# Two cross-attentions on one core: four products of the first output pair put beside the last attention subtiles, its bias added by VectorE, and two kinds of transfer changing queues

## The chip, the core and the metric

The kernel runs on one core of one Trainium2 chip. A core has TensorE (PE in the profile, with its weight loads as PEld), VectorE (DVE), ScalarE (ACT), GpSimd (POOL) and SyncE (SP, which here only issues transfers); sixteen DMA engines move data between the core's on-chip memory and the chip's main memory (DRAM). Every engine takes its own instructions strictly in order and waits on semaphores for the others. A transfer is issued by an instruction of some engine's queue, so a transfer that has to wait also holds up what stands behind it in that queue. The metric is the device time of one execution in microseconds (us), lower is better.

## The reference

Two cross-attention layers run one after the other over x of 4 x 1024 rows of 1024 numbers, float32, with a context of 64 rows for each batch item:

```python
# layer 0: 32 query heads of 32, 8 key heads, then a layer norm
q = hidden_state @ Wq + bq
scores = einsum('bkgld,bksd->bkgls', q, k) * scale + mask
attn = softmax(scores)
out = einsum('bkgls,bksd->bkgld', attn, v)  ->  (b, l, 1024)
out = out @ Wo + bo
x = out + hidden_state
return (x - mu) * rsqrt(var + EPS) * gamma + beta
# layer 1: 16 heads of 64, keys and values from the normalized context
Q = hidden_states @ Wq.T ; K = a @ Wk.T ; V = a @ Wv.T
out = softmax(Q K^T * scale) V
return hidden_states + tanh(gate) * (out @ Wo.T)
```

## The kernel before, in words

The 4096 rows are cut into 32 subtiles of 128 rows (`t`), four blocks of eight subtiles (`blk`), and 16 pairs of subtiles (`pair`). The large products (1024 x 1024 weights) are done by a scheme of seven products of half-size blocks instead of eight, so each needs sums of blocks of its two factors first: `right_sums` (L179) makes those of a weight, `left_out` (L417) makes S1, S2, S4 and, in place, S3 of a pair of subtiles with four VectorE operations. `project` (L428) runs the seven products of a pair: each is four matmuls of 128x128 by 128x512 (L436) into one of the four PSUM banks `wx`, followed by an addition of the bank into the rows `r` by VectorE (L444). Several products run on in one bank (X), so the next of them waits for the addition that reads the bank. Between the products `project` takes steps from the list `fill`.

The program has these stages.

1. Keys and values of the context, and the queries of block 0 (up to about 200 us of the profile).
2. Attention of layer 0, subtile by subtile, in `mix` (L764). A subtile has its scores (`front`, L676 on TensorE and L680 on VectorE, twice), the maxima (L687), the subtraction (L690), the exponentials (L702), the sums and reciprocals (L707, L708), the division (L711), a transposition of the probabilities, and the products with the values (`values`, L752), whose result is stored to `oTd` (L758). For subtiles from 19 on, the transposition is done by TensorE (`turn`, L406) with a copy by ScalarE (L407). Queries are loaded a subtile ahead into two buffers (`load_queries`, L643, with the mask at L647), from SP's queue.
3. Beside the attention, `mix` takes steps of `other_work` (L950) at five places of a subtile. For subtiles 0 to 23 these are the query products of the next blocks. For the last eight subtiles they are the *folded query weights* of layer 1: for each of eight chunks `k`, `turned_chunk` (L875) loads a chunk of the turned weight `wq1T` (on GpSimd's queue, L877), and four steps of `folded_queries` (L880) multiply it with the keys (L890), copy the result by ScalarE (L896) and, after each second step, store 1 MB of it to `ad` (on SP's queue, L902). Eight of the 32 steps are run ahead of subtile 24; the other 24 are three for each subtile. During chunks 1 to 4 the weight `wo` of layer 0's output is loaded; after chunk 5 its sums are made and `load_outputs(0)` (L933) loads pair 0's attention output `o2_0` and its two tiles of rows of x, to which **GpSimd** adds the bias `bo` (L946). When all steps are done, `left_out` makes pair 0's sums.
4. The output stage: a loop over the 16 pairs (L1069) runs `project` with `wo`. Its `fill` holds, for pairs 0 to 7, the *folded values* of layer 1 (`folded_values`, L908: L917 on TensorE, L922 on ScalarE, stores at L926), the closing layer norm of the pair before (`close_rows`, L1028), and in pair 0 first what is left of subtile 31 (its transposition and `values`) and `open_stage` (L1013), which gives the memory of the attention pools to the output stage's pools (`left`, `o2`, `res`, `const2`). Rows of later pairs get their bias from GpSimd (L946).
5. Layer 1, pair by pair (from about 1150 us), with no part in the change.

The order inside an engine is set by a scheduler from program order and from what each step needs, except where `keep_in_program_order` pins an instruction. The pool `wpool` has seven buffers of the tag `wb` that are used in rotation; from chunk 0 on, the chunks of `wq1T` and the two result tiles `a_k_0`, `a_k_1` of each chunk take turns in them, so a chunk's load waits for the store of a result tile of two to three chunks before (L877 and L902 depend on each other in this way).

Of the kernel before, what the change touches and what calls it, by code (L numbers as in the profile page):

```python
# [8 lines left out]
F32 = mybir.dt.float32  # L9
# [5 lines left out]
P = 128  # L15
# [56 lines left out]
def tile_two_cross_attentions(  # L72
# [352 lines left out]
        nc.vector.tensor_tensor(s["S4"], a12, s["S2"], ALU.subtract)  # L425
        return {"A11": a11, "A12": a12, "A22": a22, "S3": a21, **s}

    def project(a, w, r, fill, bias=None, tail=None):  # L428

        fresh = set()

        def product(bank, s, m, first, last):
            for k in range(HK):
                nc.tensor.matmul(  # L436
                    bank, a[s][:, k, :], w[m][:, k, :],
                    start=first and k == 0, stop=last and k == HK - 1, skip_group_check=True,
                )

        def add(u, n, bank):
            at = r[u][:, n * 512 : (n + 1) * 512]
            if bias is None or (u, n) in fresh:
                nc.vector.tensor_tensor(at, bank, at, ALU.add)  # L444
            else:
                fresh.add((u, n))
                at = at.rearrange("p (h s) -> p h s", s=S)
                nc.vector.tensor_tensor(  # L448
                    at, bank.rearrange("p (h s) -> p h s", s=S),
                    bias.unsqueeze(1).to_broadcast([P, 512 // S, S]), ALU.add,  # L450
                )

        share = -(-len(fill) // 7)

        def others():
            for _ in range(min(share, len(fill))):
                fill.pop(0)()

        X, V = wx(), wx()
        product(X, "A11", "B11", True, False)  # L460
        add(0, 0, X)
        others()
        product(X, "S2", "T2", False, False)
        add(1, 0, X)
        others()
        product(V, "S3", "T3", True, False)
        add(1, 1, V)
        others()
        product(X, "S1", "T1", False, False)
        add(1, 1, X)  # L470
        others()
        product(X, "S4", "B22", False, True)
        add(0, 1, X)
        others()
        if tail:
            tail()
        product(V, "A22", "N4", False, True)
        add(1, 0, V)
        others()
        W = wx()  # L480
        product(W, "A12", "B21", True, True)
        add(0, 0, W)
        others()

    def softmax_front(s, floor, name, late=False):
        mx = small.tile([P, 16], F32, tag="mx", name=f"mx_{name}")
# [387 lines left out]

    def turned_chunk(k):  # L875
        t = wpool.tile([P, KC, P], F32, tag="wb", name=f"wq1T_{k}")
        nc.gpsimd.dma_start(out=t, in_=wq1T[k])  # L877
        return t

    def folded_queries(kT, wT, k):  # L880

        st = [wpool.tile([P, B, 512], F32, tag="wb", name=f"a_{k}_{n}") for n in range(2)]

        def heads(cc):
            banks = [wx(), wx()]
# [14 lines left out]
            if cc % 2:  # L900
                n = cc // 2
                nc.sync.dma_start(  # L902
                    out=ad[:, sub_ap(k), n * 512 : (n + 1) * 512].rearrange("b p o -> p b o"), in_=st[n]
                )

        return [lambda cc=cc: heads(cc) for cc in range(4)]

    def folded_values(vT, wch, c):  # L908
# [21 lines left out]

        return [lambda bp=bp: keys(bp) for bp in range(2)]

    def load_outputs(pair):  # L933
        o = (o2pool if pair else early).tile([P, KC, 2 * P], F32, tag="o2", name=f"o2_{pair}")
        load = nc.sync.dma_start(out=o, in_=oTd[pair])
        if not pair:
            tc.keep_in_program_order(load)
        r = []
        for u in range(2):
            t = pair * 2 + u  # L940
            ru = (rpool.tile([P, H], F32, tag="r", name=f"r_{t}") if pair
                  else early.tile([P, H], F32, tag="r", name=f"r_{t}", bufs=2))
            load = nc.sync.dma_start(out=ru, in_=x[sub_ap(t), :])
            if not pair:
                tc.keep_in_program_order(load)
            nc.gpsimd.tensor_tensor(ru, ru, bo_sb, ALU.add)  # L946
            r.append(ru)
        return o, r

    def other_work(rows):  # L950

        nonlocal fold, early, bo_sb, w_o, first_outputs
        for blk in range(1, NBLK):
            steps = query_steps(blk, rows)
            fills = {}
# [30 lines left out]
        first_outputs = left_out(o, early, "0_0"), r  # L986

    fold_cm, early_cm = ExitStack(), ExitStack()
    fold = early = bo_sb = w_o = first_outputs = None
    work = other_work(rows)  # L990


# [9 lines left out]
        n = 28 - AHEAD if t // SUB == NBLK - 2 else 28  # L1002
        mix(t, (t % SUB + 1) * n // SUB - t % SUB * n // SUB)
    go_on(FOLD_AHEAD)
    n = 4 * KC - FOLD_AHEAD
    for i in range(SUB):
        mix(last + i, (i + 1) * n // SUB - i * n // SUB)
    next(work, None)
# [46 lines left out]

        return [lambda: half(0), lambda: half(1), blocks]

    ahead_a, ahead_r = first_outputs
    wch = chunk(wo1, 0, "wo1")

    def load_second():
        nonlocal ahead_o, ahead_r
        ahead_o, ahead_r = load_outputs(1)


    ahead_o = None
    flip, values = turned.pop(NSUB - 1)
    fill = [lambda: (flip(0), flip(1)), lambda: (values(), open_stage()), load_second]
    for pair in range(NPAIR):  # L1069
        r, a = ahead_r, ahead_a  # L1070
        if 0 < pair < NPAIR - 1:
            ahead_o, ahead_r = load_outputs(pair + 1)
        if pair < KC:
            ahead_w = chunk(wo1, pair + 1, "wo1") if pair + 1 < KC else None
            fill += folded_values(vT, wch, pair)
            wch = ahead_w
        if pair == KC + 1:
# [3 lines left out]
        if pair == 2:  # L1081
# [186 lines left out]
```

## Time and profile before

| | us |
|---|---|
| three runs: median (lowest to highest) | 1927.82 (1925.83 to 1929.95) |
| the profiled execution | 1927.79 |
| its span, first to last instruction | 1926.0 |
| TensorE busy in the span | 1866.6 |
| TensorE busy from 600 to 700 us | 72.8 |
| VectorE busy from 600 to 700 us | 92.5 |

The span and the profiled execution's own time differ by 1.8 us, which lie around the span. The mean granted clock of TensorE is 0.991 of full speed over the whole span. In windows of 50 us, TensorE is busy 47 us or more of every window but 600 to 650 us (36.97) and 650 to 700 us (35.84) and the last one, in which the span ends, and the granted clock falls there to 0.90 and 0.80; these are the last eight attention subtiles. In the windows from 1200 us to 1850 us it is busy all 50 us. A row of the stretch view lists for each stretch the busy time of every engine with the number of its instructions, then the granted clock of TensorE, the busy share of the DMA engines and the data rate. A timeline row gives start, duration, engine, line, operation, the tiles, how many instructions are merged, and in brackets the idle time in front of them with what ended it.

### The profile page before, as it was taken

What the parts mean: (1) busy time and instruction counts of PE and PEld (TensorE: products, weight loads), DVE (VectorE), ACT (ScalarE), POOL (GpSimd) and SP (SyncE); (2) the same over time, 40 slices, a digit from 0 to 9 for tenths busy, and PEclk for the clock granted to TensorE, in tenths of its full rate; (3) what the DMA queues carried; (4) which work ended last, traced back from release to release, by engine and by line L of the source; (5) the groups of instructions that cost most, each with busy time, mean ns of one, the idle gap of its engine ahead of it and who ended that gap; (6) DMA issues with size and microseconds to landing.
All of it is one profiled execution on the core that took longest, in us unless ns stands there. A gap on an engine that the chain in (4) does not pass through costs nothing.

```text
span 1926.0 us, 17427 instructions
## 1 busy us (share of the span) xinstructions
PE 1866.6 (97%) x6096; PEld 878.4 (46%) x6096; DVE 1298.3 (67%) x1580; ACT 418.8 (22%) x1316; POOL 173.6 (9%) x206
## 2 busy tenths in 40 slices
PE   8999999999998879999999999999999999999999
PEld 7744444444445543433444444444444444444444
DVE  3425589788888974665577777557665766576653
ACT  1101565766546632121100001000000000000000
POOL 0015111111100012111112200000000000000000
PEclk9999999999999979999999999999999999999999
DMA  8996599897868875676663344465756575647421
GB/s 277 184 225 184 158 258 257 255 276 233 251 176 289 280 239 180 194 237 193 198 191 142 121 118 111 109 164 140 166 140 166 138 168 138 168 136 170 120 87 44
DMA packets 224840, 350.53 MB, mean 182 GB/s; under 512 B 26992, under 2 KB 146160, under 8 KB 219760
## 3 DMA queue, kind: packets, MB, share of 16 engines
q1 hardware_dynamic: 160192, 255.03, 47.1%
q0 software_dynamic: 12016, 48.25, 8.8%
q10 hardware_dynamic: 52544, 46.14, 8.7%
q8 instruction: 48, 0.79, 0.2%
q14 instruction: 40, 0.33, 0.1%
HBM read 207.53 MB, written 141.82 MB: 181 GB/s over the span
## 4 chain that ended last, share of the span: by engine, by line
PE 83%; DVE 10%; DMA 3%; issue 2%; ACT 1%; POOL 0%; DVEq 0%; SPq 0%; ACTq 0%; POOLq 0%
PE wx L436 58%; PE wx L572 15%; PE big L676 2%; PE wx L379 1%; PE big L379 1%; PE big L917 1%; DVE s L680 1%; DVE s L711 1%; PE big L752 1%; DMA p<-s 1%; PE big L406 1%; DVE sm L707 1%; DMA pq<-p 1%; DVE mx L687 1%; PE wx L890 1%
## 5 line engine op out<-in xcount | busy, mean ns | idle before, releaser
L444 DVE TENSOR_TENSOR r<-wx,r 128x512 f32<-128x512 f32 x224 | 153.3, 686 | 239.2 <-PE wx L436 226.3
L498 ACT ACTIVATE s<-s 128x1024 f32<-128x1024 f32 x32 | 33.7, 1057 | 651.8 <-DVE s L497 651.8
L694 ACT ACTIVATE s<-s,mx 128x64 f32<-128x64 f32 x456 | 152.1, 335 | 63.3 <-DVE mx L687 59.2
L448 DVE TENSOR_TENSOR s<-wx,key_bias 128x512 f32<-128x512 f32 x64 | 44.2, 690 | 136.7 <-PE wx L436 134.0
L436 PE MATMUL wx<-wo_B,S 128*128 128x512 f32 x256 | 117.2, 600 | 2.3 <-DVE r L444 2.3
L572 PE MATMUL wx<-xT,wq_S 128*128 128x512 f32 x256 | 116.5, 598 | 0.8 <-ACT z L583 0.8
L436 PE MATMUL wx<-b_B,pT 128*128 128x512 f32 x256 | 115.8, 593 | 0.6 <-ACT pT L407 0.6
L436 PE MATMUL wx<-b_B,S_p 128*128 128x512 f32 x256 | 116.0, 596 | 0.0
L436 PE MATMUL wx<-a_B,xT 128*128 128x512 f32 x256 | 115.4, 592 | 0.0
L436 PE MATMUL wx<-a_B,S_x 128*128 128x512 f32 x256 | 115.3, 593 | 0.1
L572 PE MATMUL wx<-xB,wq_A 128*128 128x512 f32 x256 | 115.1, 597 | 0.0
L436 PE MATMUL wx<-wo_B,o 128*128 128x512 f32 x256 | 114.6, 595 | 0.0
L946 POOL TENSOR_TENSOR r<-r,bo 128x1024 f32<-128x1024 f32 x32 | 80.8, 2531 | 368.4 <-DMA r<-in_x_dram 275.1
L680 DVE TENSOR_TENSOR s<-big,m 128x1024 f32<-128x1024 f32 x64 | 77.4, 1211 | 31.9 <-PE big L676 30.2
L676 PEld LDWEIGHTS big<-kv,q 64*128 64x128 f32 x1024 | 69.2, 195 | 51.1 <-issue 45.0
L676 PE MATMUL big<-kv,q 64*128 64x128 f32 x1024 | 80.0, 291 | 7.6 <-DMA q<-qTd 7.5
L694 ACT ACTIVATION_READ_ACCUMULATOR s<-s,mx 128x1 f32 x456 | 85.4, 187 | 0.0
L711 DVE TENSOR_TENSOR s<-s,sm 128x1024 f32<-128x1024 f32 x64 | 81.1, 1274 | 0.9
L412 DVE STREAM_TRANSPOSE pT<-pq 128x1024 f32<-128x1024 f32 x66 | 78.0, 1220 | 3.0 <-DMA pq<-p 3.0
L436 PEld LDWEIGHTS wx<-wo_B,S 128*128 128x128 f32 x256 | 47.0, 190 | 69.4 <-issue 51.5
L299 ACT ACTIVATE rstd<-rstd 128x1 f32<-128x1 f32 x32 | 6.5, 203 | 324.2 <-DVE rstd L298 324.2
L436 PEld LDWEIGHTS wx<-wo_B,o 128*128 128x128 f32 x256 | 48.0, 190 | 63.5 <-issue 62.7
(158 smaller groups left out, 2941.3 us busy)
## 6 DMA issues: line engine op xcount, KB each, us to landing
p<-s POOLq DMA_DIRECT2D x19, 1024.0 KB, 6.9
pq<-p POOLq DMA_DIRECT2D x76, 256.0 KB, 5.9
xq<-in_x_dram SPq DMA_DIRECT2D x64, 256.0 KB, 10.2
q<-qTd SPq DMA_DIRECT2D x32, 512.0 KB, 6.5
oTd<-oT ACTq DMA_DIRECT2D x32, 512.0 KB, 6.7
ad<-a SPq DMA_DIRECT2D x16, 1024.0 KB, 6.8
o<-oTd SPq DMA_DIRECT2D x16, 1024.0 KB, 5.0
r<-in_x_dram SPq DMA_DIRECT2D x32, 512.0 KB, 5.4
```

Source lines behind the costliest of these rows:

```text
L379: nc.tensor.matmul(ps[:, 0:256], w[k // HK, c // HK][:, k % HK, sub_ap(c % HK)], ct[:, k, :], start=(k == 0), stop=(k == KC - 1),)
L412: return nc.vector.transpose(dst.rearrange("p k (u i) -> p k u i", i=Q), t[:, :, k0 * Q : k1 * Q].rearrange("p u (k j) -> p k u j", j=Q),)
L436: nc.tensor.matmul(bank, a[s][:, k, :], w[m][:, k, :], start=first and k == 0, stop=last and k == HK - 1, skip_group_check=True,)
L444: nc.vector.tensor_tensor(at, bank, at, ALU.add)
L448: nc.vector.tensor_tensor(at, bank.rearrange("p (h s) -> p h s", s=S), bias.unsqueeze(1).to_broadcast([P, 512 // S, S]), ALU.add,)
L498: nc.scalar.activation(s, s, AF.Exp)
L572: nc.tensor.matmul(bank, w_q[a][:, k, sub_ap(i)], rows[b][:, k, :], start=first and k == 0, stop=last and k == HK - 1, skip_group_check=True,)
L676: nc.tensor.matmul(ps[:, at : at + P], q[on, c * 4 + g, :], k0bd[on, b, c, :], start=True, stop=True,)
L680: nc.vector.tensor_tensor(quarters[:, :, c * 8 : (c + 1) * 8], ps.rearrange("p (k a l) -> p a k l", a=NQ, l=Q), mask.rearrange("p e (h l) ...
L694: nc.scalar.activation(heads[:, e, k], heads[:, e, k], AF.Exp, bias=mx[:, e, k : k + 1], accum_out=sm[:, e, k : k + 1],)
L711: nc.vector.tensor_tensor(heads[:, e], heads[:, e], wide(sm[:, e]), ALU.mult)
L946: nc.gpsimd.tensor_tensor(ru, ru, bo_sb, ALU.add)
```

## The change

The seven products of a pair become a list of steps that `products` makes, one step being a product and its addition, and `project` runs through that list. The first four steps of pair 0 (A11·B11, S2·T2, S3·T3, S1·T1) become further steps of `other_work`, behind the folded query weights, so that the last eight subtiles now share 28 steps instead of 24 (three and four in turn) and subtile 31 holds the four products. The other three products stand around the rest of subtile 31: S4·B22, its transposition, A22·N4, its `values` and `open_stage`, then A12·B21.

```diff
-    def project(a, w, r, fill, bias=None, tail=None):
+    def products(a, w, r, bias=None, tail=None):
...
+        order = [
+            ("X", "A11", "B11", True, False, 0, 0),
+            ("X", "S2", "T2", False, False, 1, 0),
+            ("V", "S3", "T3", True, False, 1, 1),
+            ("X", "S1", "T1", False, False, 1, 1),
+            ("X", "S4", "B22", False, True, 0, 1),
+            ("V", "A22", "N4", False, True, 1, 0),
+            ("W", "A12", "B21", True, True, 0, 0),
+        ]
+        return [lambda o=o: step(*o) for o in order]
...
     def turned_chunk(k):
-        nc.gpsimd.dma_start(out=t, in_=wq1T[k])
+        nc.sync.dma_start(out=t, in_=wq1T[k])
...
     def folded_queries(kT, wT, k):
-                nc.sync.dma_start(
+                nc.gpsimd.dma_start(
                     out=ad[:, sub_ap(k), n * 512 : (n + 1) * 512].rearrange("b p o -> p b o"), in_=st[n]
...
     def load_outputs(pair):
-            nc.gpsimd.tensor_tensor(ru, ru, bo_sb, ALU.add)
+            if pair:
+                nc.gpsimd.tensor_tensor(ru, ru, bo_sb, ALU.add)
...
             if k == 5:
                 run(right_sums(w_o))
-                o, r = load_outputs(0)
-
-        first_outputs = left_out(o, early, "0_0"), r
+                o, first_rows = load_outputs(0)
+                a = left_out(o, early, "0_0")
+        second = load_o(1, wpool, "wb")
+
+        def tail():
+            nonlocal ahead_a
+            ahead_a = left_out(second, early, "0_1")
+
+        first = products(a, w_o, first_rows, None, tail)
+        for _ in range(FIRST):
+            first.pop(0)()
+            yield
...
-    n = 4 * KC - FOLD_AHEAD
+    n = 4 * KC - FOLD_AHEAD + FIRST
...
+    first.pop(0)()
+    flip(0)
+    flip(1)
+    first.pop(0)()
+    values()
+    open_stage()
+    _, ahead_r = load_outputs(1)
+    run(first)
+
+    fill = [
+        lambda u=u: nc.vector.tensor_tensor(first_rows[u], first_rows[u], bo_sb, ALU.add) for u in range(2)
+    ]
+    fill += close_rows(0, first_rows)
+    for pair in range(1, NPAIR):
```

Four more things follow from it. The loads of `wq1T` chunks (eight of 512 KB) stand in SP's queue and the stores to `ad` (sixteen of 1 MB) in GpSimd's. Pair 0's bias is two VectorE operations among the `fill` of pair 1, ahead of the pair's layer norm. Pair 1's attention output is loaded into a `wb` buffer while subtile 31 runs, and its sums go to the pool `early`, which is closed one pair later. The folded values move one pair on, to pairs 1 to 8, and the load of the first folded query weights of layer 1 with them, to pair 10.

More of the change, by code (lines that the diff above doesn't have):

```diff
@@ L426, in left_out, with product, add @@
         return {"A11": a11, "A12": a12, "A22": a22, "S3": a21, **s}
-    def project(a, w, r, fill, bias=None, tail=None):
+    def products(a, w, r, bias=None, tail=None):
         fresh = set()
-        def product(bank, s, m, first, last):
+        banks = {}
+        def product(name, s, m, first, last):
+            if first:
+                banks[name] = wx()
             for k in range(HK):
                 nc.tensor.matmul(
-                    bank, a[s][:, k, :], w[m][:, k, :],
+                    banks[name], a[s][:, k, :], w[m][:, k, :],
                     start=first and k == 0, stop=last and k == HK - 1, skip_group_check=True,
                 )
-        def add(u, n, bank):
+        def add(u, n, name):
+            bank = banks[name]
             at = r[u][:, n * 512 : (n + 1) * 512]
@@ L451, in add, with step, project @@
                 )
+        def step(name, s, m, first, last, u, n):
+            if s == "A22" and tail:
+                tail()
+            product(name, s, m, first, last)
+            add(u, n, name)
+        order = [
[8 more added lines that the diff above has]
+        return [lambda o=o: step(*o) for o in order]
+    def project(a, w, r, fill, bias=None, tail=None):
         share = -(-len(fill) // 7)
-        def others():
+        for step in products(a, w, r, bias, tail):
+            step()
             for _ in range(min(share, len(fill))):
                 fill.pop(0)()
[L459 to L483, printed above, removed]
     def softmax_front(s, floor, name, late=False):
@@ L931, in folded_values, with load_o @@
         return [lambda bp=bp: keys(bp) for bp in range(2)]
+    def load_o(pair, pool, tag="o2"):
+        o = pool.tile([P, KC, 2 * P], F32, tag=tag, name=f"o2_{pair}")
+        load = nc.sync.dma_start(out=o, in_=oTd[pair])
+        if pair < 2:
+            tc.keep_in_program_order(load)
+        return o
     def load_outputs(pair):
[L934 to L937, printed above, removed]
+        o = load_o(pair, o2pool) if pair > 1 else second if pair else load_o(0, early)
         r = []
@@ L950, in other_work @@
     def other_work(rows):
-        nonlocal fold, early, bo_sb, w_o, first_outputs
+        nonlocal fold, early, bo_sb, w_o, first, first_rows, second
         for blk in range(1, NBLK):
@@ L983, in other_work @@
                 run(right_sums(w_o))
-                o, r = load_outputs(0)
-        first_outputs = left_out(o, early, "0_0"), r
+                o, first_rows = load_outputs(0)
[8 more added lines that the diff above has]
+            yield
     fold_cm, early_cm = ExitStack(), ExitStack()
-    fold = early = bo_sb = w_o = first_outputs = None
+    fold = early = bo_sb = w_o = first = first_rows = second = ahead_a = ahead_r = None
+    FIRST = 4
     work = other_work(rows)
@@ L1056, in turn_x1 @@
         return [lambda: half(0), lambda: half(1), blocks]
-    ahead_a, ahead_r = first_outputs
     wch = chunk(wo1, 0, "wo1")
[L1061 to L1066, printed above, removed]
     flip, values = turned.pop(NSUB - 1)
-    fill = [lambda: (flip(0), flip(1)), lambda: (values(), open_stage()), load_second]
-    for pair in range(NPAIR):
+    first.pop(0)()
[11 more added lines that the diff above has]
+    for pair in range(1, NPAIR):
         r, a = ahead_r, ahead_a
-        if 0 < pair < NPAIR - 1:
+        if pair + 1 < NPAIR:
             ahead_o, ahead_r = load_outputs(pair + 1)
-        if pair < KC:
-            ahead_w = chunk(wo1, pair + 1, "wo1") if pair + 1 < KC else None
-            fill += folded_values(vT, wch, pair)
+        if pair <= KC:
+            ahead_w = chunk(wo1, pair, "wo1") if pair < KC else None
+            fill += folded_values(vT, wch, pair - 1)
             wch = ahead_w
-        if pair == KC + 1:
+        if pair == KC + 2:
             w_a, w_a_sums = right_weight(ad[0], "wb", "a0", True)
@@ L1080, in tile_two_cross_attentions @@
             fill += w_a_sums[0:2] if pair == NPAIR - 3 else w_a_sums[2:4]
-        if pair == 2:
+        if pair == 3:
             early_cm.close()
```

## The prediction

> **What bounds the kernel now.** The page's first part comes first: TensorE sets the time nearly everywhere, so only what it loses counts, and section 2 of the page places the loss between 600 and 710 us. The stretch view, cut at VectorE's second score addition (L680) of each subtile, says who sets the pace there. Its columns: stretch, length, busy time of PE, PEld, DVE, ACT and POOL with their instructions, granted clock, DMA share, GB/s.
>
> ```profile
> PE 1866.6 (97%) x6096; PEld 878.4 (46%) x6096; DVE 1298.3 (67%) x1580; ACT 418.8 (22%) x1316; POOL 173.6 (9%) x206
> ...
> 600.00:612.00 12.00, 4.47 (x41) 2.62 (x40) 8.15 (x9) 6.57 (x10) 0.54 (x1) 0.86 1.09 370
> 616.26:628.19 11.93, 9.60 (x96) 6.79 (x92) 11.86 (x13) 9.01 (x14) 0.54 (x1) 1.00 0.88 279
> 652.03:663.95 11.92, 10.21 (x87) 7.79 (x88) 11.85 (x13) 7.14 (x10) 0.00 (x0) 0.86 0.74 225
> 663.95:681.79 17.84, 9.67 (x93) 6.80 (x92) 16.81 (x15) 9.04 (x14) 5.62 (x2) 0.86 1.02 339
> 681.79:695.15 13.36, 10.39 (x88) 7.64 (x86) 12.96 (x16) 8.02 (x12) 0.00 (x0) 0.76 0.28 92
> 695.15:707.95 12.80, 10.33 (x48) 6.08 (x49) 10.71 (x13) 5.96 (x8) 0.00 (x0) 0.77 0.86 277
> 707.95:737.45 29.50, 29.50 (x97) 13.88 (x98) 6.59 (x10) 9.22 (x13) 10.32 (x5) 0.95 0.80 282
> ```
>
> A subtile takes 11.92 us, of which VectorE works 11.85: it sets the pace from 616 to 708 us, and TensorE takes over at 707.95. Three stretches are longer than the pace. The timelines of SP, TensorE, VectorE and GpSimd, in that order, say why:
>
> ```profile
> 590.62 6.24 SPq L902 DMA_DIRECT2D ad<-a  x4
> 596.95 7.74 SPq L643 DMA_DIRECT2D q<-qTd  x2
> ```
> ```profile
> 611.28 2.08 PE L676 MATMUL big<-kv,q 64*128 64x128 f32 x16 [7.53 <-DMA q<-qTd]
> ...
> 664.29 2.02 PE L406 MATMUL big<-ident,s 128*128 128x128 f32 x16
> ...
> 681.33 3.70 PE L406 MATMUL big<-ident,s 128*128 128x128 f32 x16 [6.70 <-DVE s L680]
> ```
> ```profile
> 613.39 1.23 DVE L680 TENSOR_TENSOR s<-big,m 128x1024 f32<-128x1024 f32 x1 [5.21 <-PE big L676]
> ...
> 674.04 6.09 DVE L711 TENSOR_TENSOR s<-s,sm 128x1024 f32<-128x1024 f32 x2
> ```
> ```profile
> 673.43 5.62 POOL L946 TENSOR_TENSOR r<-r,bo 128x1024 f32<-128x1024 f32 x2 [27.91 <-DMA r<-in_x_dram]
> ```
>
> First, subtile 25's queries are issued only at 596.95, behind four 1 MB stores for which SP had to wait, and land 14.2 us later (the chain of waits has them at 611.1); VectorE stands 5.21 us, and 0.51 more before its next L680. Second, two divisions that take 2.35 us elsewhere (691.68) take 6.09 while GpSimd adds pair 0's bias: 3.74 us lost. Third, from 695 us on TensorE waits for VectorE and afterwards has six of pair 0's seven products still to do.
>
> **The change part by part.**
>
> *Stores to GpSimd, weight loads to SP.* In the changed program's order of instructions SP now has queries 24, a `wq1T` load, queries 25. That load needs a buffer whose reader is done (GpSimd issued it at 576.14 before), so the queries go out near 590.7 instead of 596.95. The four stores run beside them from another queue, with the DMA engines saturated (share 1.09), so I expect 8 to 11 us of landing, between the 6.5 median and the 14.2 seen: 599 to 602. VectorE needs them near 607 (its last work before the gap ends at 608.18). Gain 5.2 + 0.5 = 5.7; at worst 14.2 us of landing again, at 605, costs nothing either. Bounds: 2 (something else is late) to 5.7. What stands behind the moved loads: a load now holds SP until a store frees its buffer, with queries behind it. The loads of chunks 4 to 7 need stores issued one to three subtiles earlier, 12 us or more, against a store's 6.8 us (L902, page part 6), so I charge nothing; if stores became slow, this is where it would show. GpSimd's issue of a 1 MB store in 2 KB pieces is not in the trace; its other issues take 0.54 to 0.57 us whatever their size, and four times that, 16 x 2.2 = 35 us, would still fit the 110 us in which GpSimd is otherwise idle.
>
> *Pair 0's bias by VectorE.* Away goes the 3.74 us stall. The 0.99 us wait for `o_0` before L422 may stay, since the sums move two subtiles earlier with their load. Two additions of 128x1024 come into pair 1; L497, the nearest row with two on-chip inputs, takes 1.22 us, so 2.4 us, beside a stage where VectorE is idle a third of the time (230.7 us busy of the 350 from 750 to 1100) and TensorE works. Uncovered they would cost 2.4.
>
> *Half a folded step more per subtile.* A step is eight matmul records of L890 (about 1.1 us) and two ScalarE copies (1.1 us). In the subtiles that get four, TensorE goes from 10.2 to 11.3 and ScalarE from 9.0 to 10.1 of 11.92 us, so VectorE keeps the pace in sum; but TensorE reaches the second score product only 0.5 us ahead of L680 (639.65 against 640.11). Bounds 0 to 1.1 us for each of subtiles 25, 27 and 29, and 0.7 more for waits on ScalarE's copies (0.74 us each in the timeline): 0 to 4. I take 1.5, nearer to nothing, because TensorE has 1.7 to 2.3 us free in those subtiles.
>
> *The four products.* I play subtile 31 through by the new order, T0 being VectorE's first L680 (692.82 on the old clock: 693.95 less the division of 1.13 that now follows it). A product takes 3.55 us (730.33 to 733.87), an addition 0.65 to 0.69. VectorE: L680, division, addition 1 (to T0+2.95), L680, maxima, subtractions (8.7), addition 2 (9.4), the sums once the exponentials are done (from 9.6 to 12.2), addition 3, division to 15.2, so 708.0 against 707.81 before. TensorE: S2·T2 from 2.95 to 6.55, transposition of subtile 30 (2.02) to 8.6, S3·T3 to 12.15, values (1.09) to 13.2, S1·T1 to 16.75, half a transposition, S4·B22 from 17.75 to 21.3, the other half to 22.3, A22·N4 to 25.85, 0.8 waiting because `values` now gets the bank that addition 6 reads, values to 27.7, A12·B21 to 31.25. Pair 1 follows without a gap only if its rows are there: their buffers lie where subtile 31's transposed probabilities were, so their load waits for `values`. Before, `values` ended at 715.87 and the first biased row was ready near 725.2 (load at 715.94, GpSimd's three additions from 722.77 taking 6.97): 9.4 us. Now only two products and one matmul (8.1 us) lie between, and the next matmul must also wait for the addition (0.7): 2.0 us lost. Pair 0 thus ends at T0+33.2 = 726.0. Before it ended at 737.41, but with 3.84 us of folded values in it (two groups of L917, 1.92 each) that now come in pair 1: 733.57. Gain 7.5, bounds 4 (the rows come 3 us later) to 10 (they are in time).
>
> The transposition is priced at 2.02. Its price after an idle stretch is 3.70, and the granted clock falls to 0.64 between 680 and 690 us; the changed TensorE has no gap over 1 us there. [...]
>
> **The sum** is against the profiled execution (1927.79; span 1926.0 and 1.8 around it, which stays; the median of the runs is the same within 0.03): 5.7 + 3.7 - 1.5 + 7.5 = 15.4, giving **1912.4 us**. From pair 1 on TensorE has the same work in the same order, so nothing is given back.
>
> **The rivals.**
>
> *The pace breaks (1920).* The extra half step or a late transfer makes TensorE or ScalarE set the pace in the four-step subtiles: the full 4 us, and of the 5.7 nothing is kept because the saturated DMA engines delay the queries by another road. For it: 1.09 of DMA share and the 0.5 us margin. Against: VectorE's 11.85 of 11.92. Gain 3.7 + 7.5 - 4 = 7.
>
> *More is hidden (1907).* Pair 1's rows are in time, the pace holds, the wait for `o_0` goes: 5.7 + 4.7 + 10 = 20.4.
>
> *Slower: GpSimd's stores land late (1940).* [...] Then a `wq1T` load waits on SP for its buffer with the next queries behind it. Chunk 6's load needs the store issued near 610 and must go out by about 638 for subtile 29's queries to be in time, so the price begins at 28 us of landing; at 35 us each of four loads holds a subtile 7 us: +28 - 15.4 = 12.6 slower. Against it: GpSimd's `wq1T` loads of 603 to 645 us landed in at most 8.7 us (median 6.6) under the same VectorE load. [...]
>
> *No change (1926).* The products are done earlier but TensorE waits as long at the hand-over, because a late `o_2` holds its sums in VectorE's queue ahead of pair 0's last addition and pair 1's: that eats 7.5, and a slow pace most of the rest. For it: those four operations do stand there. Against: `o` landed 5.3 us after its issue before (711.45 to 716.74), and 8.2 are there.
>
> **How the numbers follow.** Chances: forecast 0.62, pace breaks 0.18, more hidden 0.08, stores late 0.07, no change 0.05. The forecast's own range is 1907 to 1918 (bounds 2, 0 to 4 and 4 to 10 not all at once); with most of the pace case the range of 8 in 10 is **1905 to 1922**. What a measurement can tell from no change is 0.2%, 3.9 us: faster 0.87, same 0.06, slower 0.07.
>
> **What would show it.** No wait of L676 for `q` near 605 us; no POOL operation and no L711 over 1.3 us before pair 1; a pace of 11.9 to 12.5 us per subtile from 598 us on; subtile 30's transposition near 2.0 us and a granted clock near 1.0 from 680 to 720; pair 1 starting near 718 with a wait of about 2 us for its rows. I am wrong if SP waits at the `wq1T` loads while a query load stands behind them, if stores land later than some 28 us, or if TensorE idles as long after pair 0 as it did before.

## The result, and the profile after

| | us |
|---|---|
| before: median of 5 runs beside it (lowest to highest) | 1927.82 (1925.83 to 1929.95) |
| after: median of 5 runs (lowest to highest) | 1920.36 (1919.35 to 1923.54) |
| ratio after / before (95% interval) | 0.9966 (0.9955 to 0.9977) |
| the profiled execution after, its span | 1919.66, 1917.9 |

The change gains 7.46 us, a little under half of the 15.4 forecast. The time lies inside the wide range of 1905 to 1922, near its upper end, but outside the forecast's own 1907 to 1918; the sum behind it does not hold. The two profiled executions differ by 8.1 us, in time and in span, so the traces can be set against each other.

The stretch view of the changed kernel, cut at VectorE's second score addition (now L677) of subtiles 24 to 31, without the stretch from 26 to 27; columns as before (stretch, length, PE, PEld, DVE, ACT, POOL with instructions, granted clock, DMA share, GB/s):

```profile
602.50:617.23 14.73, 10.39 (x91) 7.69 (x89) 12.10 (x13) 8.80 (x14) 0.84 (x2) 0.88 1.06 394
617.23:629.40 12.17, 10.43 (x104) 7.95 (x100) 12.07 (x13) 9.14 (x15) 1.83 (x3) 1.00 1.00 334
641.26:658.72 17.46, 11.70 (x107) 8.48 (x105) 14.41 (x17) 10.45 (x17) 2.26 (x3) 0.97 1.02 355
658.72:670.65 11.93, 9.40 (x80) 6.56 (x80) 11.86 (x14) 7.91 (x12) 0.75 (x1) 0.76 0.63 206
670.65:685.42 14.77, 12.41 (x92) 10.06 (x94) 12.18 (x13) 8.25 (x12) 1.33 (x2) 0.77 0.95 313
685.42:697.95 12.53, 10.82 (x87) 6.50 (x83) 12.46 (x13) 6.95 (x10) 0.93 (x2) 1.00 0.85 307
697.95:725.10 27.15, 27.02 (x113) 12.99 (x114) 20.12 (x26) 9.27 (x11) 0.00 (x0) 1.00 0.39 136
```

VectorE still keeps its pace of 11.9 us where nothing holds it (658.72 to 670.65), and three stretches are still longer: 14.73 us to subtile 25's scores, 17.46 us to subtile 28's, 14.77 us to subtile 30's. The first was 17.88 us before (598.38 to 616.26), the second is new (11.92 before), the third was 17.84 us. The timelines of SP, GpSimd, TensorE and VectorE, in this order, say what holds them (start, duration, engine, line, operation, tiles, idle time ahead and what ended it):

```profile
594.51 0.53 SPq L640 DMA_DIRECT2D q<-qTd  x1
...
643.46 0.44 SPq L932 DMA_DIRECT2D o<-oTd  x1
```
```profile
594.10 0.76 POOL L899 DMA_DIRECT2D ad<-a  x1 [65.42 <-ACT a L893]
...
599.98 0.75 POOL L899 DMA_DIRECT2D ad<-a  x1 [1.21 <-ACT a L893]
```
```profile
612.61 1.47 PE L673 MATMUL big<-kv,q 64*128 64x128 f32 x16 [3.64 <-DMA q<-qTd]
...
677.00 1.13 PE L887 MATMUL wx<-kT,wq1T 64*128 64x256 f32 x4 [1.83 <-ACT a L893]
```
```profile
654.04 0.69 DVE L422 TENSOR_TENSOR S<-o 128x512 f32<-128x512 f32 x1 [2.98 <-DMA o<-oTd]
...
682.25 1.22 DVE L677 TENSOR_TENSOR s<-big,m 128x1024 f32<-128x1024 f32 x1 [0.54 <-PE big L673]
685.42 1.23 DVE L677 TENSOR_TENSOR s<-big,m 128x1024 f32<-128x1024 f32 x1 [1.95 <-PE big L673]
```

Queries 25 go out 2.4 us earlier than before (594.51 against 596.95) and still make TensorE wait until 612.61: they took 18.0 us to land. Four stores to `ad` went out beside them from GpSimd's queue, one just ahead of them and three behind, and took 9.8 to 12.7 us. Pair 0's four sums now stand ahead of subtile 28's second score addition in VectorE's order, and VectorE waits 2.98 us there for an `o_0` that took 10.6 us to land. Subtile 30's scores come late, behind folded steps that waited for ScalarE.

The end of pair 0 went as forecast, or better. TensorE's timeline from subtile 31 on:

```profile
698.09 3.70 PE L439 MATMUL wx<-wo_T,S 128*128 128x512 f32 x8 [1.51 <-DVE r L448]
701.62 1.91 PE L406 MATMUL big<-ident,s 128*128 128x128 f32 x16
...
716.81 3.60 PE L439 MATMUL wx<-wo_N,o 128*128 128x512 f32 x8
720.34 1.09 PE L749 MATMUL wx<-pT,kv 64*32 64x512 f32 x16
721.36 7.13 PE L439 MATMUL wx<-wo_B,o 128*128 128x512 f32 x16
...
730.04 3.70 PE L439 MATMUL wx<-wo_T,S 128*128 128x512 f32 x8 [0.68 <-DVE r L448]
```

The 16 matmul records from 721.36 on are pair 0's last product and pair 1's first. No wait stands before L749, and pair 1's rows cost 0.68 us (TensorE waits for an addition into them, which waited for GpSimd's bias).

To compare traces I use marks. A mark is VectorE's second score addition of a subtile, in us after that of the kernel before, less the same difference at subtile 21, which lies ahead of everything that is changed (there the changed kernel is already 2.12 us late; over all runs below this offset lies between -0.28 and +2.66 us, so it belongs to the run and not to the kernel; a mark is from one execution, and two executions of one program, e2 and e14, differ by up to 1.4 us in it). T0 is the prediction's: VectorE's first score addition of subtile 31, less the 1.13 us of a division where that division still stands ahead of it (before, e1, e8, e12 and e13). The last column is the span from T0 to the end. "The swap" is the exchange of queues between the stores and the `wq1T` loads; "late sums" and the other names are those of the experiments.

| kernel | 24 | 25 | 28 | 30 | T0 | T0 to end |
|---|---|---|---|---|---|---|
| before | 0 | 0 | 0 | 0 | 0 | 1233.2 |
| changed | +2.00 | -1.15 | +4.57 | +1.51 | +0.20 | 1222.8 |
| e1 no product ahead | +1.76 | -0.48 | -0.48 | -4.26 | -4.82 | 1231.6 |
| e2 late sums | +1.71 | +0.19 | +0.61 | -2.77 | -4.08 | 1222.8 |
| e3 swap undone | 0.00 | -0.03 | +0.38 | -0.42 | -1.74 | 1223.4 |
| e4 bias on GpSimd | +1.95 | -0.49 | +7.14 | +2.56 | +1.25 | 1226.4 |
| e5 = e2, queries 25 early | +9.54 | +3.59 | +5.11 | +1.79 | +0.48 | 1227.2 |
| e6 = e2, swap undone | 0.00 | +0.24 | +0.64 | -2.72 | -4.03 | 1222.1 |
| e7 = e6, queries 25 early | 0.00 | -3.95 | +1.45 | -1.87 | -3.18 | 1223.0 |
| e8 = before, queries 25 early | 0.00 | -3.80 | -3.81 | -3.84 | -3.85 | 1232.5 |
| e9 = e2, half of the swap | +9.60 | +3.65 | +7.62 | +4.30 | +2.99 | 1223.1 |
| e10 = e6, 12 steps ahead | +5.90 | +8.57 | +8.57 | +4.90 | +5.59 | 1218.3 |
| e11 = e7, 12 steps ahead | +11.36 | +5.41 | +5.41 | +1.75 | +3.78 | 1216.9 |
| e12 = e7, even steps | +0.64 | -3.79 | -3.80 | -9.72 | -8.87 | 1229.6 |
| e13 = e2, even steps | +2.11 | -0.22 | -0.22 | -6.13 | -5.30 | 1226.3 |
| e14 = e2 again | +1.80 | -1.20 | +1.74 | -1.57 | -2.89 | 1222.8 |
| e15 = e6 again | 0.00 | +0.08 | +1.60 | -1.71 | -3.03 | 1222.1 |

So, by the marks, the whole gain of the changed kernel lies behind T0 (10.4 us). Ahead of it, where the forecast had a gain of 7.9 us (5.7 + 3.7 - 1.5), nothing is left.

### The profile page after: what moved, and what is told of

It is laid out like the page before. It is cut to its first block, busy times and chain, and to the rows that moved or that the text cites. A ratio compares the mean times of both kernels' runs of the same rounds, so it can differ in the third digit from the quotient of the medians.

```text
span 1917.9 us, 17437 instructions
## 1 busy us (share of the span) xinstructions
PE 1867.4 (97%) x6096; PEld 877.4 (46%) x6096; DVE 1296.9 (68%) x1582; ACT 419.2 (22%) x1316; POOL 178.4 (9%) x212
## 4 chain that ended last, share of the span: by engine, by line
PE 83%; DVE 6%; issue 5%; DMA 3%; ACT 1%; POOL 1%; DVEq 0%; ACTq 0%; POOLq 0%; SPq 0%
PE wx L439 58%; PE wx L569 15%; PE big L673 2%; DMA pq<-p 2%; PE big L914 1%; PE wx L379 1%; PE big L379 1%; PE big L749 1%; DMA p<-s 1%; DVE s L677 1%; DVE pT L412 1%; DVE s L708 1%; PE big L406 1%; DVE mx L684 0%; ACT b L919 0%
## 5 line engine op out<-in xcount | busy, mean ns | idle before, releaser
L677 DVE TENSOR_TENSOR s<-big,m 128x1024 f32<-128x1024 f32 x64 | 77.5, 1212 | 31.7 <-PE big L673 29.7
L439 PEld LDWEIGHTS wx<-a_B,S_x 128*128 128x128 f32 x256 | 48.5, 190 | 62.0 <-issue 58.4
## 6 DMA issues: line engine op xcount, KB each, us to landing
xq<-in_x_dram SPq DMA_DIRECT2D x64, 256.0 KB, 10.2
```

Source lines behind the costliest of these rows:

```text
L439: nc.tensor.matmul(banks[name], a[s][:, k, :], w[m][:, k, :], start=first and k == 0, stop=last and k == HK - 1, skip_group_check=True,)
L677: nc.vector.tensor_tensor(quarters[:, :, c * 8 : (c + 1) * 8], ps.rearrange("p (k a l) -> p a k l", a=NQ, l=Q), mask.rearrange("p e (h l) ...
```

## The experiments

Each run's median stands beside the median of the kernel before on the same chip, then the ratio with its 95% interval.

### Each part of the change taken back alone

*e1: no product ahead.*

```diff
-    FIRST = 4
+    FIRST = 0
```

> The changed kernel with no product ahead of time: pair 0's seven products all come after the last folded step, the last eight subtiles share 24 steps again; queue swap, VectorE bias and early sums stay. Theory (all of the measured gain comes from the products, and the rest of the change nets to nothing in the attention tail): 1920.4 + 10.3 for the products, less up to 2.5 because the scores of subtile 30 are no longer late behind four folded steps: 1928 to 1931. Rival (the products were worth the 7.5 of the forecast or less, less the 1.5 to 2.5 of their extra half steps, and the rest of the change gains something): 1923 to 1926.

Measured: 1921.86 against 1928.25, ratio 0.9966 (0.9953 to 0.9978), the same as the changed kernel with its products. The theory was wrong by 6 us or more, the rival by 1.1. The products are worth 1231.6 - 1222.8 = 8.8 us behind T0, but the changed kernel is 5.0 us later at T0 than this one (+0.20 against -4.82). With three steps for each subtile, chunk 5 ends a subtile later, the scheduler puts pair 0's sums into subtile 29, and they wait for nothing.

*e2: late sums.* The first of the four sums is pinned in VectorE's order after chunk 6 instead of being placed freely after chunk 5; the load stays where it was.

```diff
-    def left_out(o, pool, name):
+    def left_out(o, pool, name, pin=False):
...
-        nc.vector.tensor_tensor(s["S1"], a21, a22, ALU.add)
+        first = nc.vector.tensor_tensor(s["S1"], a21, a22, ALU.add)
+        if pin:
+            tc.keep_in_program_order(first)
...
-                a = left_out(o, early, "0_0")
+            if k == 6:
+                a = left_out(o, early, "0_0", True)
```

> The changed kernel with pair 0's four sums pinned in VectorE's order two subtiles later (ahead of subtile 30's second score addition instead of subtile 28's), so that VectorE no longer stands 2.98 us waiting for o_0, and the 2.5 us of sums fall where it waited 1.95 us for subtile 30's scores. Theory (VectorE's order sets the end up to its first score addition of subtile 31): 3 to 5 us faster than the changed kernel, 1915.5 to 1917.5, no wait at L422. Rival (TensorE is as late for another reason, so the wait comes back at the scores of the next subtiles): 1919.5 to 1921.

Measured: 1915.82 against 1928.25, ratio 0.9935 (0.9922 to 0.9947), 4.5 us faster than the changed kernel by the medians and 6.0 by the ratios. VectorE's timeline of this kernel at subtile 30 (L679 is its score addition):

```profile
676.41 0.68 DVE L422 TENSOR_TENSOR S<-o 128x512 f32<-128x512 f32 x1
677.02 1.22 DVE L679 TENSOR_TENSOR s<-big,m 128x1024 f32<-128x1024 f32 x1
678.15 0.68 DVE L425 TENSOR_TENSOR S<-S,o 128x512 f32<-128x512 f32 x1
...
679.95 1.22 DVE L679 TENSOR_TENSOR s<-big,m 128x1024 f32<-128x1024 f32 x1
```

No row has a wait. The sums cost their 2.5 us and no more, T0 comes 4.3 us earlier (-4.08 against +0.20), and everything behind T0 stays as it was (1222.8 both). 2.98 us of that is the wait itself. The other 1.3 us is no more than a difference of two executions: e14, the same program again, has T0 at -2.89, 3.1 us earlier than the changed kernel. The theory holds.

*e3: the queue swap undone.*

```diff
-        nc.sync.dma_start(out=t, in_=wq1T[k])
+        nc.gpsimd.dma_start(out=t, in_=wq1T[k])
...
-                nc.gpsimd.dma_start(
+                nc.sync.dma_start(
                     out=ad[:, sub_ap(k), n * 512 : (n + 1) * 512].rearrange("b p o -> p b o"), in_=st[n]
```

> The changed kernel with the stores of the folded query weights back on SP and the wq1T loads back on GpSimd. Theory: queries 25 go out behind four stores again (3.2 us more of waiting at subtile 25, 0.6 back at 24), and o_0's load now stands behind stores in SP's queue while its sums stay ahead of subtile 28's score addition, so the wait of 2.98 us grows: 1923 to 1932. Rival (the DMA engines are saturated, so which queue a transfer has makes no difference): 1919.5 to 1921.5.

Measured: 1915.99 against 1928.25, ratio 0.9944 (0.9931 to 0.9956). Neither theory nor rival: taking the swap back made the kernel 4.4 us faster by the medians, 1.3 us by the marks. The 5.25 us wait for queries 25 came back, as expected, but mark 25 is no later than before (-0.03), and the sums moved a subtile down by themselves, where `o_0` cost 1.14 us. So this run changes two things; e6 separates them.

*e4: pair 0's bias on GpSimd again.*

```diff
-            if pair:
-                nc.gpsimd.tensor_tensor(ru, ru, bo_sb, ALU.add)
+            nc.gpsimd.tensor_tensor(ru, ru, bo_sb, ALU.add)
...
-    fill = [
-        lambda u=u: nc.vector.tensor_tensor(first_rows[u], first_rows[u], bo_sb, ALU.add) for u in range(2)
-    ]
-    fill += close_rows(0, first_rows)
+    fill = close_rows(0, first_rows)
```

> The changed kernel with pair 0's bias added by GpSimd again, right after its rows land, and not by VectorE in pair 1. Theory (two divisions or other VectorE operations run some 3.7 us longer beside GpSimd, in subtiles 28 to 30 where VectorE sets the pace): 1923.5 to 1925. Rival (the contention falls into VectorE's waits of subtile 28 or 30, 2.98 and 1.95 us, and pair 1 is spared two VectorE additions): 1919.5 to 1921.5.

Measured: 1923.71 against 1928.25, ratio 0.9981 (0.9972 to 0.9990); by the ratios 2.9 us slower than the changed kernel (0.0015 of 1927.8). The timelines of GpSimd and VectorE:

```profile
654.76 5.10 POOL L947 TENSOR_TENSOR r<-r,bo 128x1024 f32<-128x1024 f32 x2 [10.95 <-DMA r<-in_x_dram]
```
```profile
654.50 1.22 DVE L677 TENSOR_TENSOR s<-big,m 128x1024 f32<-128x1024 f32 x1
655.63 2.03 DVE L423 TENSOR_TENSOR S<-S,o 128x512 f32<-128x512 f32 x1
657.59 2.83 DVE L424 TENSOR_TENSOR o<-o 128x512 f32<-128x512 f32 x1
```

What runs longer beside GpSimd is now two of the sums: 2.03 and 2.83 us where one takes 0.69, 3.5 us in all, while L677, one of whose inputs lies in PSUM, keeps its 1.22 us. The theory's time holds, its path only in part. T0 is 1.05 us later than in the changed kernel (+1.25 against +0.20), since VectorE's waits for `o_0` (1.38 instead of 2.98) and for subtile 30's scores (1.07 instead of 2.49) are shorter, as the rival had it. The other 3.6 us are lost behind T0 (1226.4 against 1222.8). VectorE's and TensorE's timelines of pair 1 show where:

```profile
737.04 1.28 DVE L309 SCALAR_TENSOR_TENSOR r<-r,rstd,beta 128x1024 f32<-128x1024 f32 x1 [2.00 <-DMA beta<-in_beta_dram]
```
```profile
738.98 5.40 PE L439 MATMUL wx<-wo_B,S 128*128 128x512 f32 x8 [2.66 <-DVE r L448]
```

Pair 0's layer norm comes earlier than in the changed kernel (L306 at 731.54 against 735.49) and waits 2.00 us for the load of `beta`; TensorE waits 2.66 us for an addition behind it, and its next product takes 5.40 us (3.60 in the changed kernel).

### Why the queries still came late

*e5: late sums, queries 25 right behind queries 24.* They were issued inside subtile 24's `mix`; now they go out ahead of the first chunk of `wq1T` in program order.

```diff
-        if (t + 1) % SUB:
+        if (t + 1) % SUB and t != NSUB - SUB:
             load_queries(t + 1)
...
+        load_queries(NSUB - SUB + 1)
         wT = turned_chunk(0)
```

> The kernel of the second experiment (late sums, swap kept) with the load of queries 25 issued right behind queries 24, ahead of the next wq1T loads in SP's queue. In the changed kernel these queries were issued at 594.51 and VectorE still stood 1.34 + 0.75 us for subtile 25's scores. Theory (place in the queue decides when they land): 1.5 to 2.5 us faster than the 1915.8 of late sums, 1913 to 1914.5. Rival (the DMA engines are saturated by the 1 MB stores beside them, so an issue 1 to 2 us earlier lands no earlier): 1915 to 1917.

Measured: 1921.31 against 1925.31, ratio 0.9976 (0.9966 to 0.9987): slower than e2, which neither had. SP's, TensorE's and VectorE's timelines of this kernel:

```profile
591.78 1.28 SPq L642 DMA_DIRECT2D q<-qTd  x2
593.36 2.89 SPq L876 DMA_DIRECT2D wq1T<-wq1T  x2
```
```profile
604.84 2.08 PE L889 MATMUL wx<-kT,wq1T 64*128 64x256 f32 x8 [6.41 <-DMA wq1T<-wq1T]
```
```profile
608.66 1.23 DVE L679 TENSOR_TENSOR s<-big,m 128x1024 f32<-128x1024 f32 x1 [8.96 <-PE big L675]
```

Queries 25 were in time, and a chunk of `wq1T`, now behind them, took their place: TensorE stands 6.41 us for it, with the second half of subtile 24's scores queued behind. Another 4.4 us are lost behind T0 (1227.2 against e2's 1222.8), where TensorE again waits in pair 1 for VectorE (1.18 and 1.38 us) and has a product of 5.40 us.

*e6: late sums, swap undone* (the edits of e2 and e3).

> The kernel of late sums with the queue swap undone, so that the swap is priced without the place of the sums. If the swap is worth the 5.7 of the forecast: 1920.5 to 1922. If it nets to nothing, because what it wins at subtile 25 it loses at 22 and 24 (theory, by the marks of the first four runs: -0.5 on average): 1914.5 to 1917.5. If it costs the 4.4 us by which the third experiment came out ahead of the changed kernel: 1910.5 to 1912.5.

Measured: 1914.97 against 1925.31, ratio 0.9953 (0.9937 to 0.9968). T0 is -4.03 against -4.08 with the swap: the swap nets to nothing. By the marks, what it wins at subtile 25 (from +1.71 to +0.19, against 0.00 to +0.24) it had lost up to subtile 24.

*e7: e6 with queries 25 early* (the edits of e2, e3 and e5; the queries now stand ahead of the four stores in SP's own queue).

> The kernel before this one with queries 25 issued ahead of the four 1 MB stores in SP's queue, the swap still undone. Theory (queue order alone was what the swap had to mend, and the swap paid for it with other waits): the wait of 5.25 us at subtile 25 goes and nothing else moves, 4 to 5.7 us faster than the kernel before this one, 1910 to 1912.5. Rival (the stores issued next delay the queries as much from behind, or the scores of subtile 26 become late instead): within 1.5 us of the kernel before this one.

Measured: 1914.20 against 1925.31, ratio 0.9941 (0.9928 to 0.9954), within 1.5 us of e6, as the rival had it. The wait at subtile 25 is gone (-3.95), but the gain is lost by subtile 28 (+1.45). The stretch view over subtile 26 of this kernel, then of e2:

```profile
620.00:632.00 12.00, 12.00 (x88) 10.29 (x96) 9.79 (x11) 7.56 (x12) 0.54 (x1) 0.72 0.94 298
```
```profile
620.00:632.00 12.00, 10.26 (x99) 7.72 (x100) 11.90 (x13) 9.52 (x16) 1.50 (x2) 1.00 0.91 273
```

Much the same work (the cut is by time, so a few matmuls differ) keeps TensorE busy for the whole 12 us at a granted clock of 0.72, and for 10.26 us at 1.00. At 0.72 VectorE idles (9.79 busy), at 1.00 it doesn't (11.90).

*e8: the kernel before, with queries 25 early and nothing else.*

> The kernel before the change with nothing but the load of queries 25 moved ahead of the four stores. It prices the forecast's largest single term alone. Forecast (a wait of 5.21 + 0.51 us removed passes to the end in full): 1922 to 1923. If the time comes back at the later wait of 6.70 us around GpSimd's bias, because o_0 and pair 0's rows keep their own time: 1925 to 1928.

Measured: 1923.65 against 1925.31, ratio 0.9989 (0.9980 to 0.9997), 0.6 to 3.9 us, between the two ranges. The marks have -3.80 at subtile 25 and -3.85 at T0: with three steps for each subtile, what the queries win passes through unchanged. SP's timeline shows how:

```profile
591.36 1.32 SPq L643 DMA_DIRECT2D q<-qTd  x2
592.77 6.93 SPq L902 DMA_DIRECT2D ad<-a  x4
```

*e9: late sums and the first half of the swap* (the edit of e2 and the first of e3's two lines, so stores on GpSimd and `wq1T` on GpSimd too).

> Late sums, and of the swap only its first half: the stores go by GpSimd, and the wq1T loads go by GpSimd as well, so SP issues queries 24, 25 and 26 with nothing between. It asks why queries 25 took some 18 us to land in the changed kernel. Theory (their packets share the DMA engines with the 1 MB stores that now run beside them, instead of standing ahead of them or behind them in one queue): issued near 592 they still land at 606 to 612, a wait of 1 to 3 us stays at subtile 25, and the time is 1914 to 1917. Rival (the wq1T loads in front of them in SP's queue made them late): no wait at subtile 25, 1911 to 1913.

Measured: 1921.57 against 1927.97, ratio 0.9967 (0.9954 to 0.9979): both were wrong on the time. TensorE's and VectorE's timelines:

```profile
606.65 2.08 PE L889 MATMUL wx<-kT,wq1T 64*128 64x256 f32 x8 [5.58 <-DMA wq1T<-wq1T]
```
```profile
610.45 1.23 DVE L679 TENSOR_TENSOR s<-big,m 128x1024 f32<-128x1024 f32 x1 [8.11 <-PE big L675]
```

Queries 25 cause no wait, and again a chunk of `wq1T` does. From 600 to 610 us the DMA engines move 376 GB/s in the kernel before, 409 in the changed one, 417 in e5, 404 here and 397 in e8, at a busy share of 1.02 to 1.07. The queries took 6.6 us to land in e8, 9.7 in e5, 13.1 here and 18.0 in the changed kernel. I read this so: with the engines busy all the time something has to be late. In e8 it is the four stores, for which nobody waits at once; with the stores in another queue it is what TensorE needs next.

### Where the last half step goes

*e10 and e11: twelve steps ahead of subtile 24 instead of eight* (e6 and e7 with `FOLD_AHEAD = 12`).

> Late sums, swap undone, and twelve instead of eight folded steps ahead of subtile 24, so that every one of the last eight subtiles has three steps and none has four. Theory (a subtile with four steps makes TensorE's next scores 2 to 3 us late wherever VectorE is otherwise on pace, as in the seventh experiment, 0.55 + 1.56 us and 0.55 + 2.03 us; the four steps put ahead cost some 4.4 us of TensorE, but in front of the 5.25 us wait for queries 25): 1 to 3 us faster than the sixth experiment's kernel, 1912 to 1914. Rival (two more 1 MB stores now stand ahead of queries 25, so that their wait moves along with the scores of subtile 24): 2 to 5 us slower than it, 1917 to 1920.

> The kernel before this one with queries 25 ahead of the stores. Theory (with neither a wait for queries nor a four-step subtile VectorE keeps its pace of 11.9 us from subtile 24 on; the four steps ahead cost 2.5 to 4.4 us there, against 3.95 for the queries and 2.46 + 2.93 us for the four-step subtiles of the seventh experiment): 1910.5 to 1913, the fastest so far. Rival (what is put ahead of subtile 24 costs its full price, because TensorE works without a pause up to there): 1913.5 to 1916.

Measured: e10 1917.85 against 1927.97, ratio 0.9945 (0.9931 to 0.9959); e11 1917.19, ratio 0.9943 (0.9931 to 0.9956). No gain that the intervals show. The marks stand still from subtile 25 to 29 (+8.57 and +5.41), so no step there costs anything, but with the four steps put ahead subtile 24 comes 5.9 us later in e10 and 11.4 in e11.

*e12 and e13: even steps* (e7 and e2, with three folded steps in each subtile and all four products in subtile 31).

```diff
-        mix(last + i, (i + 1) * n // SUB - i * n // SUB)
+        mix(last + i, 3 + FIRST * (i == SUB - 1))
```

> Late sums, swap undone, queries 25 ahead of the stores (the seventh experiment's kernel) with the steps shared out otherwise: three folded steps in each of the last eight subtiles, and all four products in subtile 31, which so has seven steps. Theory (the 3.95 us that the early queries win are lost again in the subtiles with four folded steps, 2.46 us in subtile 26's interval and 2.93 us in 28's, where TensorE also works at a granted clock of 0.72): the gain of 3.9 us holds until subtile 30, subtile 31 pays some 3.3 us for the three folded steps that are now in it, 1911 to 1913. Rival (subtile 31 pays as much as the others win, or some other wait takes the place): 1914 to 1916.5.

> The same sharing out with the swap kept and no early queries (late sums otherwise). Theory: as the late sums kernel lost nothing in its four-step subtiles before subtile 30 (granted clock 1.00 there), the even steps win nothing there and subtile 31 pays up to 3.3 us for its three folded steps: 1915 to 1919. Rival (four-step subtiles cost 1 to 2 us each whatever the clock): 1911 to 1914.

Measured: e12 1917.33 against 1926.18, ratio 0.9957 (0.9944 to 0.9971); e13 1917.73, ratio 0.9959 (0.9946 to 0.9971). In e12 VectorE waits for nothing from subtile 25 to T0, which comes 8.87 us earlier than before; but behind T0 the kernel takes 1229.6 us, 6.6 more than e7. Three folded steps now lie there (some 3.3 us), and the second product waits and runs at a lower rate, as TensorE's timeline shows (5.40 us instead of 3.70):

```profile
694.63 5.40 PE L441 MATMUL wx<-wo_T,S 128*128 128x512 f32 x8 [2.05 <-DVE r L450]
```

Both ranges of e12 were missed, the rival's (1914 to 1916.5) by 0.8 us; its reason fits the marks, as subtile 31 pays what the others win. For e13 the theory's time holds (1917.73 in 1915 to 1919), though not its reason: T0 comes 1.2 us earlier than in e2, and 3.5 us are lost behind it.

*e14 and e15: e2 and e6 again, on one chip.*

> The second experiment's kernel again, on the same chip as the next one: the two differ in the queue swap alone. If the swap is worth the forecast's 5.7 us, this one is 5 to 6 us faster than the next; if it nets to nothing, as the marks of subtile 31 had it (-5.21 against -5.16 us), within 2 us of it.

> The sixth experiment's kernel again, beside the one before on the same chip: within 2 us of it if the swap nets to nothing, 5 to 6 us slower than it if the swap is worth the forecast's 5.7 us, 2 to 4 us faster if the swap costs time.

Measured: e14 1916.33 against 1926.18, ratio 0.9953 (0.9940 to 0.9965); e15 1914.57, ratio 0.9949 (0.9936 to 0.9963); T0 -2.89 and -3.03. The swap is worth nothing that these runs can measure, and not the 5.7 us of the forecast.

The version with late sums is faster than before in both runs (0.9935 and 0.9953) and than the changed kernel (0.9966) clearly in e2; in e14 the intervals overlap. Undoing the swap on top of it, with or without early queries (e6, e7, e15: 0.9953, 0.9941, 0.9949), makes no further difference that the intervals allow to be told; early queries with the swap kept (e5: 0.9976) are slower.

## Why the prediction was wrong

By the marks, in us of gain, the forecast and the trace stand so:

| place | forecast | trace |
|---|---|---|
| up to subtile 24 | 0 | -2.0 |
| subtile 25 (queries) | +5.7 | +3.1 |
| subtiles 26 to 28 (`o_0` and its sums) | 0 | -5.7 |
| subtiles 29 and 30 (bias, late scores) | +3.7 - 1.5 | +3.1 |
| subtile 31 up to T0 | 0 | +1.3 |
| behind T0 | +7.5 | +10.4 |
| sum | 15.4 | 10.2 |

Less the 2.1 us by which this execution was late already at subtile 21, the 10.2 are the 8.1 us between the two profiled executions.

*The step that failed is the first one, the queue swap.* The prediction had the queries "go out near 590.7" and expected "8 to 11 us of landing, between the 6.5 median and the 14.2 seen". It held that even 14.2 would cost nothing. They went out at 594.51, which is 592.4 without the run's own offset of 2.1, and took 18.0 us. So their place in the queue came out nearly as forecast, and the price of the stores that run beside them did not: it was set between two landings that had been seen while the stores stood in SP's own queue. I read the busy DMA engines (share 1.09 in the prediction's own first stretch) as the obstacle: stores in GpSimd's queue take them up as well, those issued after the queries included. From 590 to 615 us of the changed kernel the packets of GpSimd's queue take 51% of the 16 engines' time and those of SP's queue 37%, and two stores issued behind the queries, at 596.06 and 598.02, land after 11.2 and 11.7 us, ahead of them. e5 and e9 bring the queries in on time and lose more at the next load. Measured at T0, the whole swap is worth 0.05 us (e2 against e6). The prediction carried such a delay only inside its rival "the pace breaks" ("the saturated DMA engines delay the queries by another road"), at a chance of 0.18.

The swap also changed what stands ahead of subtile 24: one of the sums of `wo` (L183, 2.28 us) moved in VectorE's order from an idle place to one on the path (before it runs at 548.51 in front of L589, which then waits 0.28 us; changed it runs at 555.37, and the same addition waits 2.46 us without it). Mark 22 is +1.35 or +1.36 in every kernel that has the whole swap and 0.00 in every kernel that has none or half of it. The prediction looked only at the last eight subtiles of that order. No run keeps the swap with L183 in its old place, so what the swap would be worth without this is open.

*The second step that failed is one that was costed at nothing.* "The 0.99 us wait for `o_0` before L422 may stay, since the sums move two subtiles earlier with their load" was the right place and the wrong size: 2.98 us, and VectorE's lateness passed on to subtile 30. It was measured alone (e2, and again as e14): 4.3 and 3.1 us by the marks, 4.5 and 4.0 us by the medians. The load took 10.6 us to land in a stretch with a DMA share of 1.02, VectorE was there 7.6 us after its issue, and the sums had no slack, as they now stood ahead of a score addition.

*The bias* was right in what it takes away: no addition of GpSimd's and no division over 1.23 us is left before pair 1. Its size, 3.74 forecast and 2.9 measured by the ratios, agrees partly by luck: in e4 the sums run 3.5 us longer, but only 1.05 us of that reaches T0, and the rest of the loss arises in pair 1. What ran longer beside GpSimd were VectorE instructions with two inputs in the core's SBUF memory: two divisions before (6.09 us instead of 2.35), two sums in e4 (2.03 and 2.83 us instead of 0.69). L677, with one such input, kept its 1.22 us in e4.

*Half a step more per subtile* (1.5, bounds 0 to 4): e1 against e2 puts it at 0.7 us at T0, and against e14 at 1.9. In the changed kernel itself subtile 30's scores are 0.54 + 1.95 = 2.5 us late. All are inside the bounds; the difference goes with the granted clock, which the prediction expected to stay near 1.0 from 680 us on and which is 0.50 there for 4 us in the changed kernel and 1.00 in e2.

*The four products* (7.5, bounds 4 to 10): 8.8 us behind T0 by e1 against e2, 6.0 us in all by their medians. The order that the prediction played through holds. S2·T2 was to start at T0 + 2.95 and does (698.09); the transposition takes 1.91 us (2.02 taken); A12·B21 was to end at T0 + 31.25 and ends, by a product of 3.55 us from 721.36, at T0 + 29.8. The wait of 0.8 us for the bank did not come, and the 2.0 us for pair 1's rows were 0.68; together that is 2.8 of the 2.9 us by which the span behind T0 beats the sum.

*The rivals.* "The pace breaks" (1920) came within half a microsecond of the measured time, which is partly luck. One of its reasons is right: of the 5.7 nothing is kept. The other, the full 4 us for the extra half steps, is not; `o_0` stands in that place, and the span behind T0 gave 2.9 us more than the sum had for the products. "Stores land late" did not happen: the stores' median landing is 9.2 us, 28 would have been needed, and GpSimd's issue takes 0.75 us, at the lower end of its bounds. (The 8.7 us that the prediction gives as the most for GpSimd's loads of 603 to 645 us is the load of 592.07; those took at most 7.6.) "No change" and "more is hidden" did not happen either.

## What to carry to other kernels

Moving a transfer to another queue changed who waits here, and little of what the DMA engines moved (376 to 417 GB/s); where their share is 1, ask which transfer may be late at no cost, and put that one last in the same queue (e8: 3.85 us at T0 in one execution, 1.7 us by the medians, from the order of two rows). When a step is shifted to an earlier place, its load is shifted too, here to a busier one (`o_0` took 10.6 us at a DMA share of 1.02): check for every reader of a load how long it had to land before, and what stands behind the reader in its engine's order. And compare the order of instructions from the first row that differs, not from the stage that is meant to change.

## What was not expected of the hardware

In these runs it goes with the granted clock whether a subtile with four steps keeps its pace. In the changed kernel the clock is 0.50 from 680 to 684 us, although TensorE has no gap longer than 1.83 us between 660 and 678 us (before, a gap of 6.70 us stood ahead of the 0.64 from 680 to 690 us); in e2 it is 1.00 from 668 to 692 us, with the same steps. It differs between executions of one program too: from 648 to 656 us it is 1.00 in e2, and 0.53 and then 0.61 in e14, which loses 2.75 us from subtile 27 to 28 where e2 loses 0.2 (the gaps ahead are alike, 1.83 and 1.82 us). The stretch from 660 to 664 us of the changed kernel, also at 0.50, has gaps of 3.37 and 1.53 us ahead of it, so the two drops there do not follow gaps of one length. What sets the clock there was not tried by itself and stays open.

Executions differ ahead of any change: e2 and e14 are one program, and at subtile 21 they are 0.93 and 1.86 us behind the profiled execution of before. The offset grows in steps of about 0.7 us: the changed kernel's is 0.67 us at 204 us, 1.45 at 304, 2.13 at 432, and then stays there to subtile 21. Where a difference of 2 us matters, a mark in an unchanged stage has to be subtracted first.
